# Expert slots padded to 128 instead of 256, in tiles of two halves, in a fused attention and mixture-of-experts layer

## The chip, the cores and the metric

The kernel runs on one NeuronCore of a Trainium2 chip, as one program and one launch. The metric is the device time of that program in microseconds. Before the change the median of three runs is 931.68 us (931.22 to 932.55). A difference is told here from medians; durations of single instructions come from one profiled execution, whose own time stands in the table below.

The core has four engines that matter here. [...] VectorE (DVE), ScalarE (ACT) and GpSimd (POOL) work element by element. Each runs its own queue of instructions in order, and waits on semaphores for the others. DMAs are issued from queues too: here almost all from SyncE's (SP), the ones with indices from POOL's.

## What is computed

The input x is 4 sequences of 1024 tokens of 128 channels, in float32. After a layer norm, an attention part and a mixture-of-experts part both read the normed rows xn, and both are added to x.

```python
x = x + attention(xn) + experts(xn)

# attention: 16 heads of 8 channels, each sequence of 1024
s = q @ k^T                                 # all columns, not only the causal ones
s = s - s.mean(-1); mad = abs(s).mean(-1) + 1e-6
s = s / mad * gain
r = max(where(causal, s, -1000), 0) ** 4
y = (r / (r.sum(-1) + 1e-6)) @ v;  y @ W_proj + b_proj

# experts: 8 experts, each token goes to its best 2, weights from a softmax over the two
z = (xn @ w1[e] + b1[e]) * (xn @ w2[e] + b2[e])          # 128 -> 256
y = silu(z @ wg[e] + bg[e]) @ w3[e] + b3[e]              # 256 -> 256 -> 128
```

There are 4096 tokens, so 8192 pairs of a token and an expert.

## The kernel before

**Order.** The program is written down by a planner (class `Plan`, before line 150). Every step (`add(...)`) names its engine or a choice of engines with a time each, the steps it depends on, the buffers it takes and gives back, and a rank. `Plan.run` repeatedly picks the step with the smallest start time, less a correction by name from the table `SOONER`, then by rank and the table `RANK`; so these tables, the times and the number of buffers of each kind (`kinds`) set the order of every engine's queue, and which engine takes a step that may run on several. Where PE would be idle, `pads` inserts a filler matmul (L1426). The order is fixed when the program is built; nothing is reordered when it runs.

**Attention.** For each of the 4 sequences (`prepare`), q and k are made channel by token (L767), and v token by channel (L873). q is scaled by a power of two that bounds it: L825 multiplies the absolute values of q by a matrix of mean absolute k, giving a bound in PSUM; L813 turns that into a power of two, written over the absolute values in SBUF (`aq`); L816 multiplies q by it. Sums of each head are then made from `aq` and q (L897, L903). k is copied four times with all but one quarter of the heads zeroed (`km`, L842). Then `chunk` handles 512 query rows at a time, two chunks in a sequence: `up` (L942) forms all scores, four heads at a time on 32 rows of the array each, whose absolute sums are drained by DVE (L955) or ACT (L957); `score` (L1066) forms the causal scores transposed, which go through a relu with the mask (L1085 on DVE; L1094 DVE, L1092 ACT), and two squarings (L1119 POOL, L1117 ACT); `relu` (L1133) and `values` (L1142) sum them and multiply by v, four heads on 32 columns of the array each; `finish` normalises, with a transpose (L1010).

**Routing.** `route` picks two experts for each token, counts the tokens of each expert, and gives each pair a slot: the slots of an expert begin at a multiple of TS = 256, so at most (8192 + 8 x 255) // 256 = 39 tiles of 256 slots are in use, and `owner` holds the expert of each tile. A 5 MB buffer in HBM (`xs`) is filled with zeros, and 64 indirect DMAs on POOL (L723) scatter the normed rows to their slots, with weight and destination beside each row.

**Experts.** `experts` goes through the 39 tiles. SP reads the tile's expert into a register and issues the rows (L1234) and the weights w1, w2, wg, w3 (L1235 to L1238), 640 KB, into one of two weight buffers. PE transposes the rows (L1247), multiplies by w1 and w2 (`up` of `experts`, L1257), ACT adds the bias (L1331), DVE adds the other bias and multiplies (L1339), PE multiplies by wg (`mix`, L1264), ACT applies silu (L1363), PE multiplies by w3 (`down`, L1273), DVE or ACT scales by the gate (L1285, L1288), and two indirect DMAs on POOL add the rows to a sum in HBM (L1293). A tile's down product and the next tile's up product are one step on PE, and so are its mix product and the next tile's transposes. These steps stand between the steps of the attention in PE's queue. At the end `collect` reads the sums back (L1381), adds them (L1390) and stores the output (L1395).

Of the kernel before, what the change touches and what calls it, by code (L numbers as in the profile page):

```python
# [9 lines left out]
I32 = mybir.dt.int32  # L10
# [16 lines left out]
TS = 256  # L27
# [24 lines left out]
class Plan:  # L52
# [6 lines left out]
    SOONER = {"score": 0.23, "mask": 0.1, "norm": 0.19, "tbias": -0.09, "count": -0.58, "v": 0.01, "top": 0.2, "wT": -0.06, "kappa": -0.11, "gateT": 0.12, "k": 0.21, "abs": -0.69, "ys": -0.51, "stats": 0.59, "exp": 0.14, "sq": -0.86, "bound": 0.53, "proj": -0.42, "least": 1.02, "xg": -0.51, "give": -0.32, "yT": -0.16, "sum": -0.3, "heads": 0.32, "gate": -0.5, "headsT": 0.15, "normal": 0.19, "second": -0.02, "relu": -0.88, "y@DVE": -0.32, "gate@DVE": 0.11, "relu@DVE": 0.45, "xT": 0.46, "xg@DVE": -0.05, "relu@ACT": 0.42, "out": -0.77, "yT@DVE": -0.19, "xT@DVE": -0.19, "place": -0.11, "gate@ACT": -0.01, "g": -0.01, "wT@ACT": 0.34, "heads@DVE": -0.33, "mean": -0.33, "y": -0.03, "abs@DVE": 0.6, "ys@DVE": -0.15, "sq@ACT": -0.11, "warm": 0.63, "xg@ACT": -0.83, "norm@ACT": 0.05, "up": 0.16, "q": 0.06, "blocks": -0.09, "ys@ACT": 0.01, "spill": -0.53, "weight": -0.46, "wT@DVE": 0.22, "gain": -0.07, "gates": 0.91, "av": -0.1}  # L59
    RANK = {"score": 221, "proj": -10, "yT": -194, "xg": -11, "sums": 48, "h": -24, "tbias": -35, "bound": -15, "top": 4, "headsT": 187, "spill": 12, "blocks": 240, "place": 4, "sum": -136, "std": -27, "gateT": 10, "count": -34, "scatter": 85, "xT": 210, "y": 196, "exp": 27, "second": -251, "load": 209, "relu": -111, "keys": 126, "mask": 6, "rows": -13, "scale": 8, "turn": 101, "wT": 23, "fill": 17, "ys": -19, "bias": -6, "g": -103, "give": -106, "gate": 36, "absq": 16, "norm": -137, "warm": -16, "v": -15, "hot": -162, "gates": 21, "stats": 20, "up": 78}  # L60
# [105 lines left out]
def layer_kernel(  # L166
# [49 lines left out]
    SB = TS // P  # L216
    N_TILES = (2 * NT + E * (TS - 1)) // TS
# [10 lines left out]
    def keep(shape, name, dtype=F32):  # L228
# [5 lines left out]
        "u": (8, [P, 2, CH]), "u1": (6, [P, 2, CH]), "blk": (14, [P, TB * WX]),  # L234
        "w": (2, [P, 2 * F + FB * F + FB * C]), "xg": (3, [P, SB, WX]), "xT": (2, [P, TS]),
        "z": (2, [P, FB, TS]), "s": (2, [P, FB, TS]), "ye": (2, [P, SB, C]),         "ys": (2, [P, CH]), "yt": (2, [P, CB, C]),
# [105 lines left out]
    tiles_f = keep([P, N_TILES], "tiles_f")  # L342
    expert_f = keep([P, 1], "expert_f")
    for t, pattern, base, cm in (
        (first, [[-1, E]], E, 0),
        (tiles_f, [[1, N_TILES]], 0, 0), (expert_f, [[0, 1]], 0, 1),
    ):
        nc.gpsimd.iota(t, pattern=pattern, base=base, channel_multiplier=cm, allow_small_or_imprecise_dtypes=True)
# [24 lines left out]
    xs = dram.tile([N_TILES * TS, WX], F32, name="xs")  # L373
# [47 lines left out]
    own = keep([E, N_TILES], "own")  # L421
    one8 = keep([P, TB], "one8")
    nc.vector.memset(one8, 1.0)
    owner = keep([P, N_TILES], "owner", I32)
    biases = keep([P, 3, FB, N_TILES], "biases")
# [130 lines left out]
    def route(rank):  # L556
# [84 lines left out]
        def owners(e):  # L641

            past = room(0, N_TILES * (E - 1)).rearrange("p (n e) -> p n e", e=E - 1)
            nc.vector.tensor_tensor(
                past, tiles_f.unsqueeze(2).to_broadcast([P, N_TILES, E - 1]),
                ends(1)[:, 1:].unsqueeze(1).to_broadcast([P, N_TILES, E - 1]), ALU.is_ge,
            )
            o0 = of_buf(k1)[:, NE + 160 : NE + 160 + N_TILES]
# [11 lines left out]
        def bias(e):  # L660
            pb = of_buf(k2)[:, : 3 * FB * N_TILES].rearrange("p (i f n) -> p i f n", i=3, f=FB)
            for i in range(3):
                for f in range(FB):
                    nc.tensor.matmul(pb[:, i, f, :], bes[:, i, f * P : (f + 1) * P], own, start=True, stop=True)
# [5 lines left out]
                biases.rearrange("p i f n -> p (i f n)"), of_buf(k2)[:, : 3 * FB * N_TILES]  # L670
# [72 lines left out]
    def prepare(b, cs, rank):  # L743
# [65 lines left out]
        def scale(here, bound):  # L809


            t = of_buf(aq)[:, here]
            nc.vector.tensor_scalar(  # L813
                t.bitcast(I32), bound.bitcast(I32), 0x7F800000, -0x1000000, ALU.bitwise_xor, ALU.bitwise_and
            )
            nc.vector.tensor_tensor(of_buf(qb)[:, here], of_buf(qb)[:, here], t, ALU.mult)  # L816

        sd = []
        for c in range(NC):
# [12 lines left out]
                    deps=[m, qd[c]], give=[k], rank=rank,  # L832
# [76 lines left out]
        m = add("heads", {"PE": 1.3}, heads, deps=sd + [bl], take=[sh[b]], give=[aq], rank=rank + 8)  # L909
# [305 lines left out]
    def experts(routed, ranks, stored):  # L1215
# [3 lines left out]
        tile_ = [{k: Buf(k) for k in ("w", "xg", "xT", "z", "s", "ye")} for _ in range(n_)]  # L1219

        def weights_of(i):
            w = of_buf(tile_[i]["w"])
# [4 lines left out]
        def loaded(i):  # L1227


            def load(e):  # L1230
                of_ = nc.sync.value_load(owner[0:1, i : i + 1], min_val=0, max_val=E - 1)
                this = bass.DynSlice(of_, 1)
                w1s, w2s, wgs, w3s = weights_of(i)
                nc.sync.dma_start(of_buf(tile_[i]["xg"]), slots_d[:, i * SB : (i + 1) * SB, :])  # L1234
# [224 lines left out]
```

## Time and profile before

| What | Value |
|---|---|
| Median of 3 runs | 931.68 us (931.22 to 932.55) |
| Profiled execution, its own time | 934.0 us |
| Its span, first to last instruction | 932.3 us |
| Granted TensorE clock, mean | 0.985 of full speed |
| PE, busy | 901.4 us |
| ACT, busy | 718.1 us |
| POOL, busy | 756.1 us |
| DVE, busy | 644.5 us |
| Moved by DMA | 58.63 MB, mean 63 GB/s |
| First expert tile's up product | 284.9 us after the start |
| Last expert tile's down product | 905.8 us |

Busy time is the union of an engine's instructions. PE's matmuls are pipelined and their records overlap, so what a burst of matmuls costs is read from its start to the start of the next one. A matmul of float32 operands stands in the trace as two records, a transpose as one. "32*128" in a record means 32 rows and 128 columns of the array; four such matmuls on different rows (or "128*32", different columns) run side by side. Line numbers are those of the kernel before; of the kernel after, its own.

### The profile page before, as it was taken

Reading aid. Unit: us, or ns where it says so; the run is one execution under the profiler, and the core shown is the slowest. Engines: PE = TensorE matmul, PEld = TensorE weight load, DVE = VectorE, ACT = ScalarE, POOL = GpSimd, SP = SyncE. Lnnn points to the kernel's source line nnn. Section 1 sums busy time; section 2 is a strip of 40 time slices with the busy share of each in tenths; the row PEclk is TensorE's granted clock in tenths of the full one; section 3 lists DMA queues with packets and bytes.
Section 4 is the critical chain, followed back from the end, with each engine's and each line's share of the span. In section 5 each row is a group of like instructions: output and inputs, shape, how many; then the busy total and the mean of one; then the engine's idle time right before and its main releaser. Section 6 shows DMA issues by size and latency. Waiting matters only on the chain.

```text
span 932.3 us, 20608 instructions
## 1 busy us (share of the span) xinstructions
PE 901.4 (97%) x7517; PEld 458.4 (49%) x7517; DVE 644.5 (69%) x1616; ACT 718.1 (77%) x1564; POOL 756.1 (81%) x519
## 2 busy tenths in 40 slices
PE   6899999998999999999899999999999999999996
PEld 4455433433454545545445654454545565544443
DVE  7888856568776766666567776665666776666565
ACT  5879888897786868678757877777787868678983
POOL 4478879889676889999957887999987838899992
PEclk9999999999898999999989999999999999999999
DMA  4820000000021233233212221232322222222106
GB/s 107 333 79 22 24 21 21 22 24 21 22 80 39 48 76 78 58 68 78 63 41 54 67 57 43 60 65 59 83 63 63 56 62 59 63 59 44 41 7 187
DMA packets 66275, 58.63 MB, mean 63 GB/s; under 512 B 6463, under 2 KB 62206, under 8 KB 66174
## 3 DMA queue, kind: packets, MB, share of 16 engines
q1 hardware_dynamic: 52168, 47.67, 16.8%
q0 software_dynamic: 13280, 9.38, 7.4%
q8 instruction: 59, 0.97, 0.4%
q10 hardware_dynamic: 726, 0.27, 0.2%
q14 instruction: 42, 0.34, 0.1%
HBM read 36.90 MB, written 20.40 MB: 61 GB/s over the span
## 4 chain that ended last, share of the span: by engine, by line
PE 83%; DVE 7%; POOL 6%; issue 2%; DMA 1%; ACT 1%; SPq 0%; ACTq 0%; POOLq 0%; DVEq 0%
PE bank L942 17%; PE bank L1066 16%; PE bank L1142 14%; PE bank L1133 9%; PE bank L1264 8%; PE bank L1257 7%; PE bank L1273 4%; POOL u L1119 4%; PE bank L1010 2%; POOL xs L723 1%; PE bank L767 1%; PE bank L1247 1%; DVE blk L816 1%; PE bank L1426 1%; DMA blk<-acc 1%
## 5 line engine op out<-in xcount | busy, mean ns | idle before, releaser
L1119 POOL TENSOR_TENSOR u<-u 128x1024 f32<-128x1024 f32 (+1 forms) x324 | 582.1, 1924 | 99.4 <-ACT u L1092 62.7
L1117 ACT ACTIVATE u<-u 128x1024 f32<-128x1024 f32 (+1 forms) x316 | 298.2, 971 | 11.7 <-POOL u L1119 5.6
L955 DVE TENSOR_REDUCE asum<-bank 128x1 f32<-128x512 f32 (+3 forms) x500 | 243.0, 543 | 62.1 <-PE bank L942 61.3
L1092 ACT ACTIVATE u<-bank 128x256 f32<-128x256 f32 (+2 forms) x355 | 152.4, 492 | 71.9 <-DVE u L1085 44.0
L942 PE MATMUL bank<-blk,blk 32*128 32x512 f32 (+3 forms) x1536 | 188.4, 529 | 7.1 <-DVE blk L816 4.7
L1085 DVE SCALAR_TENSOR_TENSOR u<-bank,causal 128x256 f32<-128x256 f32 (+1 forms) x384 | 121.2, 372 | 89.6 <-PE bank L1066 70.9
L1066 PE MATMUL bank<-blk,blk 32*128 32x512 f32 (+3 forms) x1536 | 178.9, 528 | 1.0 <-DVE u L1085 0.5
L1142 PE MATMUL bank<-u,V 128*32 128x512 f32 (+3 forms) x1536 | 165.1, 501 | 1.6 <-POOL u L1119 1.3
L957 ACT ACTIVATE bank<-bank 128x512 f32<-128x512 f32 (+3 forms) x268 | 130.5, 488 | 35.1 <-PE bank L942 31.8
L1293 POOL DMA_INDIRECT acc<-ye,xg x78 | 123.0, 1577 | 36.6 <-DVE ye L1285 20.5
L1094 DVE TENSOR_SCALAR u<-bank 128x512 f32<-128x512 f32 (+2 forms) x157 | 98.9, 656 | 55.9 <-PE bank L1066 55.9
L942 PEld LDWEIGHTS bank<-blk,blk 32*128 32x128 f32 x1536 | 90.6, 185 | 86.1 <-issue 13.5
L1133 PE MATMUL bank<-u,pick 128*32 128x512 f32 (+3 forms) x1280 | 129.1, 469 | 0.0
L1066 PEld LDWEIGHTS bank<-blk,blk 32*128 32x128 f32 x1536 | 65.7, 184 | 72.5 <-issue 27.1
L1133 PEld LDWEIGHTS bank<-u,pick 128*32 128x32 f32 x1280 | 43.6, 111 | 79.3 <-issue 74.5
L723 POOL DMA_INDIRECT xs<-blk,slot x64 | 64.5, 1008 | 21.4 <-DMA xs<-blk,slot 11.2
L1264 PE MATMUL bank<-z,w 128*128 128x256 f32 x312 | 77.1, 390 | 0.0
L1142 PEld LDWEIGHTS bank<-u,V 128*32 128x32 f32 x1536 | 33.9, 108 | 83.4 <-issue 58.3
L1257 PE MATMUL bank<-xT,w 128*128 128x256 f32 x312 | 74.7, 383 | 0.0
L1264 PEld LDWEIGHTS bank<-z,w 128*128 128x128 f32 x312 | 56.1, 190 | 25.9 <-issue 8.8
L1257 PEld LDWEIGHTS bank<-xT,w 128*128 128x128 f32 x312 | 56.9, 193 | 7.7 <-DVE asum L955 1.5
L1339 DVE SCALAR_TENSOR_TENSOR z<-bank,biases,z 128x256 f32<-128x256 f32 x78 | 37.2, 478 | 30.8 <-ACT z L1331 30.7
(176 smaller groups left out, 700.5 us busy)
## 6 DMA issues: line engine op xcount, KB each, us to landing
w<-in_L_ffn_w_dram SPq DMA_DIRECT2D x117, 128.0 KB
w<-in_L_ffn_wg_dram SPq DMA_DIRECT2D x39, 256.0 KB
xs<-w SPq DMA_DIRECT2D x1, 5070.0 KB
xg<-xs SPq DMA_DIRECT2D x39, 130.0 KB
acc<-w SPq DMA_DIRECT2D x1, 2048.0 KB
blk<-acc SPq DMA_DIRECT2D x4, 512.0 KB
out_dram<-xt SPq DMA_DIRECT2D x8, 256.0 KB
xt<-in_L_attn_x_dram SPq DMA_DIRECT2D x3, 512.0 KB
```

Source lines behind the costliest of these rows:

```text
L942: nc.tensor.matmul(of_buf(ks_[g])[:, at : at + w], of_buf(q[b])[rows_, ii * P : (ii + 1) * P], of_buf(km[b][r])[rows_, k0 : k0 + w], start ...
L955: nc.vector.tensor_reduce(to, of_, AX.X, ALU.add, apply_absolute_value=True)
L957: nc.scalar.activation(of_, of_, AF.Abs, accum_out=to)
L1066: nc.tensor.matmul(of_buf(ks_[g])[:, at : at + n], of_buf(km[b][r])[rows_, jj * P : (jj + 1) * P], of_buf(q[b])[rows_, c * CH + off : (c + ...
L1092: nc.scalar.activation(to, s_, AF.Relu)
L1117: nc.scalar.activation(to, s_, AF.Square)
L1119: (nc.vector if e == "DVE" else nc.gpsimd).tensor_tensor(to, s_, s_, ALU.mult)
L1133: nc.tensor.matmul(of_buf(acc)[32 * g : 32 * g + 32, off + lo : CH], pick, of_buf(u1s[g // 2])[:, g % 2, at + lo : at + n], start=begin, s ...
L1142: nc.tensor.matmul(of_buf(acc)[32 * g : 32 * g + 32, off:CH], of_buf(Vb[b])[:, jj, h0 : h0 + 32], of_buf(us[g // 2])[:, g % 2, at : at + n ...
L1257: nc.tensor.matmul(of_buf(k)[:, j * TS : (j + 1) * TS], wt[:, f * P : (f + 1) * P], of_buf(tile_[i]["xT"]), start=True, stop=True)
L1264: nc.tensor.matmul(of_buf(k)[:, g * TS : (g + 1) * TS], weights_of(i)[2][:, f, g * P : (g + 1) * P], of_buf(tile_[i]["z"])[:, f, :], start ...
L1293: nc.gpsimd.indirect_dma_start(out=acc_d, in_=of_buf(ye)[:, j, :], in_offset=None, compute_op=ALU.add, out_offset=bass.IndirectOffsetOnAxi ...
```

## The change

- TS becomes 128. A tile still has 256 slots, but in two halves (SB = 2) that may belong to different experts. There are at most 71 halves, so 36 tiles, and `owner`, `own`, `biases` and the zeroed buffer are sized by the 72 halves.
- Each half has weights and biases of its own: there are four weight buffers for two, a tile loads 2 x 640 KB, each 256-wide matmul of `up` and `mix` becomes two 128-wide ones with their own weights, and each instruction with a bias becomes two.
- Rows and weights are loaded by separate steps of the plan; the transpose waits for the rows alone, and the up product for the weights.
- In `scale`, the power of two is written in place in PSUM and multiplied into q from there; a new step copies it to `aq`, and the per-head sums wait for the copy.
- The kind "blk" has 11 buffers for 14, and the tables `SOONER` and `RANK` have other values, so that the whole program has another order, and some steps run on another engine.

```diff
-TS = 256
+TS = 128
-    SOONER = {"score": 0.23, "mask": 0.1, "norm": 0.19,
...
+    SOONER = {"score": 0.41, "v": 0.2, "wT": -0.2,
...
-    N_TILES = (2 * NT + E * (TS - 1)) // TS
+    SB = 2
+    TW = SB * TS
+    N_TILES = -(-((2 * NT + E * (TS - 1)) // TS) // SB)
+    N_OWN = N_TILES * SB
...
-        "u": (8, [P, 2, CH]), "u1": (6, [P, 2, CH]), "blk": (14, [P, TB * WX]),
-        "w": (2, [P, 2 * F + FB * F + FB * C]), "xg": (3, [P, SB, WX]), "xT": (2, [P, TS]),
+        "u": (8, [P, 2, CH]), "u1": (6, [P, 2, CH]), "blk": (11, [P, TB * WX]),
+        "w": (4, [P, 2 * F + FB * F + FB * C]), "xg": (3, [P, SB, WX]), "xT": (2, [P, TW]),
...
-            t = of_buf(aq)[:, here]
-            nc.vector.tensor_scalar(
-                t.bitcast(I32), bound.bitcast(I32), 0x7F800000, -0x1000000, ALU.bitwise_xor, ALU.bitwise_and
-            )
-            nc.vector.tensor_tensor(of_buf(qb)[:, here], of_buf(qb)[:, here], t, ALU.mult)
+            t = bound.bitcast(I32)
+            nc.vector.tensor_scalar(t, t, 0x7F800000, -0x1000000, ALU.bitwise_xor, ALU.bitwise_and)
+            nc.vector.tensor_tensor(of_buf(qb)[:, here], of_buf(qb)[:, here], bound, ALU.mult)
...
+            ts.append(
+                add(
+                    "bound", {"ACT": 0.58, "DVE": 0.62}, lambda e, k=k, here=here: copy(e, of_buf(aq)[:, here], of_buf(k)),
+                    deps=[sd[-1]], give=[k], rank=rank,
+                )
+            )
...
-        m = add("heads", {"PE": 1.3}, heads, deps=sd + [bl], take=[sh[b]], give=[aq], rank=rank + 8)
+        m = add("heads", {"PE": 1.3}, heads, deps=ts + [bl], take=[sh[b]], give=[aq], rank=rank + 8)
...
+            def rows_(e):
+                nc.sync.dma_start(of_buf(tile_[i]["xg"]), slots_d[:, i * SB : (i + 1) * SB, :])
+
             def load(e):
...
+                for j in range(SB):
+                    n = i * SB + j
+                    of_ = nc.sync.value_load(owner[0:1, n : n + 1], min_val=0, max_val=E - 1)
...
+            return (
+                add(
+                    "rows_in", {"SP": 0.6}, rows_, deps=routed, take=[tile_[i]["xg"]], rank=ranks[i] - 20, after=3.0,
+                    begin=max(0.0, ranks[i] - 20),
+                ),
+                add(
+                    "load", {"SP": 4.6}, load, deps=routed, take=tile_[i]["w"], rank=ranks[i] - 20, after=5.0,
+                    begin=max(0.0, ranks[i] - 20),
+                ),
+            )
...
         def up(i, f, k):
-            for j, wt in enumerate(weights_of(i)[:2]):
-                nc.tensor.matmul(
-                    of_buf(k)[:, j * TS : (j + 1) * TS], wt[:, f * P : (f + 1) * P], of_buf(tile_[i]["xT"]), start=True, stop=True
-                )
+            for m in range(2):
+                for j in range(SB):
+                    nc.tensor.matmul(
+                        of_buf(k)[:, m * TW + j * TS : m * TW + (j + 1) * TS], weights_of(i, j)[m][:, f * P : (f + 1) * P],
+                        of_buf(tile_[i]["xT"])[:, j * TS : (j + 1) * TS], start=True, stop=True,
+                    )
...
+                def first(e, i=i, f=f, k=k):
+                    for j in range(SB):
+                        at, n = slice(j * TS, (j + 1) * TS), i * SB + j
+                        nc.scalar.activation(
+                            of_buf(tile_[i]["z"])[:, f, at], of_buf(k)[:, at], AF.Identity, bias=biases[:, 0, f, n : n + 1]
+                        )
...
+                h = add("h", {"ACT": 0.46}, first, deps=[m] + zd[:1], rank=rank - 200)
+                zd.append(add("h", {"DVE": 0.46}, product, deps=[h], give=[k], rank=rank - 200))
...
-            s_ready = add("g", {"ACT": 0.74}, silu, deps=[m], give=[k], rank=rank - 200)
+            s_ready = add("g", {"ACT": 0.9}, silu, deps=[m], give=[k], rank=rank - 200)
```

The `mix`, product and silu steps are split into halves in the same way.

## The prediction

> **What bounds the kernel now.** I read the page first (shares, chain), then the stretches by time, then one expert tile in the timeline, and last the waits of TensorE.
>
> ```profile
> PE 901.4 (97%) x7517; PEld 458.4 (49%) x7517; DVE 644.5 (69%) x1616; ACT 718.1 (77%) x1564; POOL 756.1 (81%) x519
> ...
> PE 83%; DVE 7%; POOL 6%; issue 2%; DMA 1%; ACT 1%; SPq 0%; ACTq 0%; POOLq 0%; DVEq 0%
> ```
>
> TensorE is busy 97% of the span and is 83% of the chain that ended last; the rest of that chain is DVE and POOL, in places. Where these places are, the stretches tell (columns: stretch, its length, busy us and count of PE, PEld, DVE, ACT, POOL, granted clock, DMA share, GB/s):
>
> ```profile
> 67.00:125.00 58.00, 57.71 (x493) 29.07 (x490) 48.24 (x118) 51.46 (x129) 47.83 (x39) 1.00 0.07 22
> 125.00:217.00 92.00, 90.39 (x739) 33.83 (x735) 56.44 (x141) 79.19 (x153) 83.14 (x63) 1.00 0.07 22
> 217.00:290.00 73.00, 68.95 (x551) 33.99 (x547) 56.09 (x123) 55.52 (x127) 56.89 (x43) 0.91 0.15 44
> 290.00:457.00 167.00, 166.02 (x1388) 86.56 (x1381) 106.83 (x262) 125.00 (x262) 148.21 (x87) 1.00 0.29 67
> 457.00:477.00 20.00, 15.03 (x72) 7.80 (x70) 17.00 (x24) 10.09 (x18) 11.79 (x9) 0.83 0.17 34
> ...
> 600.00:906.00 306.00, 305.79 (x2622) 159.54 (x2619) 202.15 (x492) 240.03 (x514) 265.77 (x159) 1.00 0.26 57
> ```
>
> From 290 on, with expert tiles mixed in, PE is full and the others have room: there a microsecond of PE work is a microsecond of time. Before the first expert tile (284.9 us) ACT is at 89% (67 to 125) or POOL at 90% (125 to 217), and PE, though "busy", moves at their pace. Around 217 to 240 and 457 to 477, where a batch's q and k are prepared, PE stands still and its clock falls to 0.91 and 0.83.
>
> One expert tile on PE (start, length to the last end, line; x8 is four fp32 matmuls of two records each):
>
> ```profile
> 404.01 0.66 PE L1010 MATMUL bank<-ident,ys 128*128 128x128 f32 x4
> 404.50 1.89 PE L1264 MATMUL bank<-z,w 128*128 128x256 f32 x8
> 406.23 0.38 PE L1247 MATMUL bank<-ident,xg 128*128 128x128 f32 x2
> 406.55 1.14 PE L1066 MATMUL bank<-blk,blk 32*128 32x512 f32 x8
> 407.62 1.16 PE L1273 MATMUL bank<-w,s 128*128 128x128 f32 x8
> 408.61 1.89 PE L1257 MATMUL bank<-xT,w 128*128 128x256 f32 x8
> 410.43 0.71 PE L942 MATMUL bank<-blk,blk 32*128 32x256 f32 x8
> ```
>
> Read start to start. The eight 256-wide records of L1264 take 406.23 - 404.50 = 1.73 us, 0.216 each. L1257 takes 1.82: the extra 0.09 is the change to the 32-row form of L942. L1273's eight 128-wide records take 0.99; less 0.10 for the change before them that is 0.89, 0.111 each. A change of array form thus costs 0.1 to 0.2 us, leaving and entering.
>
> **The change, part by part.**
>
> *Fewer tiles, narrower matmuls.* Slots padded to 128: (8192 + 8 x 127) // 128 = 71 halves, so 36 tiles for 39. A tile now costs 0.89 (down) + 1.73 (up) + 1.73 (mix) + 0.22 (transposes) = 4.57 us; after, up and mix are 16 records of 128 each, 16 x 0.1115 = 1.78, and the tile 4.68. 39 x 4.57 = 178.2; 36 x 4.68 = 168.5: **-9.7 us**, all on PE, which has nothing to hide it behind. The doubt is the step of a 128-wide record with weights of its own. The row first: L1273 is that case already, a new stationary operand for each 128-wide matmul, at 0.111. [...] I take the row, since it is the same array, type and shape; between 0.108 and 0.115 the term lies between -13.7 and -5.7.
>
> *Replanned order.* In the built order of PE the changes of array form fall from 586 to 565 (rows to full array -10, columns to rows -12, columns from full -8, others +9). By the 0.1 to 0.2 us above, about 0.18 on average: **-3.8**. Filler matmuls are 16 for 17: nothing.
>
> *q times its power of two.* L816 multiplied two SBUF tiles; now the power of two is made in PSUM in place and the multiply reads it there, and a new copy (ACT or DVE) brings it to SBUF for the per-head sums.
>
> ```profile
> L816 DVE TENSOR_TENSOR blk<-blk,blk x8: 691/693/4174, 32.4 to 695.4; 128x512 f32<-128x512 f32 x8
> ...
> PE bank L942 <- DVE blk L816: 4.7, 2, 3.3
> ...
> 226.08 2.74 DVE blk L816
> ...
> 463.75 4.18 DVE blk L816
> ```
>
> Five of eight take 0.69 us, three take 2.74, 2.73 and 4.17, each beside a POOL square; L881 and L1208, of the same size with one operand in PSUM, average 0.68 and 0.69. So 2.05 + 2.04 + 3.48 = 7.6 us of DVE go. On PE: the 4.7 above, and 2.0 at 232.57 behind the second multiply, 6.7 in all. The halved clock that follows the standstills costs more: (1 - 0.83) x 20 = 3.4 at 457, (1 - 0.91) x 73 = 6.6 at 217. But the standstills have other causes too that stay (L797 2.51 us at 222.69, L805 2.82 at 458.92), so I credit little of that: **-8**, from -3 to -14. The eight copies of about 0.6 us (L435's 512-wide form 0.588, on ACT) are not ahead of the scores: only the per-head sums wait for them, and for these only the first head turn. What is late if they slip is that turn, and behind it the release of aq.
>
> *Rows apart from weights.* The built SP queue still runs rows, weights, weights, tile by tile, so a weight load still stands behind the rows' wait for an earlier scatter-add:
>
> ```profile
> SPq L1234 <- DMA acc<-ye,xg: 364.5, 36, 11.7
> ```
>
> Today this wait costs PE nothing: in the trace the rows of tile i+3 are issued 12 to 14 us after tile i's down product begins. In the new order the densest tiles are 12 to 14 us apart, and the transpose of those rows comes at the end of the mix of tile i+2, some 19 to 23 us after. Behind the rows come two weight sets, eight issues 0.58 us apart and two register loads of about 1 us: 6.7 us, so they start at about 13, end near 20 (the last waits for the next down product anyway) and are wanted at 26 or later. Bytes: 36 x 1.31 MB for 39 x 0.66, in the dense stretch 1.3 MB per 13 us = 100 GB/s more or less, where the second slice of the page moved 333. **0**, up to +2 for each of 22 dense tiles if scatter-adds come 6 us later than now.
>
> *Chain inside a tile.* Up to mix is ACT, DVE, ACT, DVE. Each 256-wide instruction (L1331 0.473, L1339 0.478) becomes two 128-wide ones with biases of their own: about 0.25 + 0.37 = 0.62 us a pair on ACT (0.473 less 128 elements at 0.83 ns, the slope between L957's forms of 512 and 128), 0.6 on DVE. [...] Now 9 us of other PE work lie between up and mix (410.43 to 419.86); in the built order of the changed kernel, with each burst at its duration in this trace, 14 of 36 tiles have just 2.6 to 3.5 us (a score, a value, a count and an up burst). A late mix holds everything behind it on PE. I take 0.3 to 0.4 us for those 14: **+5**, from 0 to +20.
>
> *Work moved to ACT.* In the built queues ACT gains 44 squares from POOL (31 of 1024, 0.95 start to start; 13 of 512, 0.52): 36 us; 82 absolute sums from DVE (0.27 for 128 to 0.60 for 512 with the read-out): 39; 20 relus: 8; and for the experts 288 x 0.25 for 156 x 0.36: 16. ACT goes from 718 to about 817 of some 920, 89%; POOL falls to about 665, DVE to about 600. In the first chunk (67 to 125), already the slowest, ACT gains about 2 us of work, while POOL, which paced 125 to 217, loses 7. Later stretches come to 85% on average, the fullest 25 us to some 95%. What waits when ACT is late is a PSUM bank, hence the next four-bank burst. 0 if the buffers even it out, +25 if ACT cannot pass the 89% it reaches at 67 to 125; nearer the former, as the 306 us from 600 ran with POOL at 87% and PE full: **+5**.
>
> *Fewer blk buffers (11 for 14), routing over 72 halves, later first tile.* DVE's placing of owners grows by 0.3 us; the tail after the last down product has the same structure. **0**, from -2 to +4.
>
> Sum: -9.7 - 3.8 - 8 + 5 + 5 = -11.5. The profiled execution took 934.0 (932.3 of span and 1.7 around it) and would become 922.5; the median of the runs lies 2.3 below it, so 931.7 becomes **920**.
>
> **Rivals.**
> 1. *The waits do not come* (chain and ACT at 0): 931.7 - 21.5 = 910. For it: the steady stretch has run without PE waits at POOL 87%. Against: the short gaps between up and mix.
> 2. *The waits eat the gain, no more*: 927 to 934. For it: first chunk, where ACT at 89% already slows PE.
> 3. *Slower: the mix waits.* Place: the mix of each tile, behind ACT's queue with 128-wide pairs. It pays 21.5 us back when the mean wait of 36 tiles reaches 0.6 us; at 0.9 it is 931.7 - 21.5 + 32 + 5 = 947. For it: ACT at 89%, strict order in its queue, a relu of 0.48 ahead of each pair. Against: 22 of 36 tiles have over 3.5 us.
> 4. *Weights or rows late* in the dense stretch, 2 us for 22 tiles: +44, about 964.
>
> **How the numbers follow.** Forecast (912 to 927 by itself) 0.58; rival 1 0.20; rival 2 0.10; rival 3 0.09; rival 4 0.03. A difference under 0.2%, 1.9 us, cannot be told from none here. Faster: 0.58 + 0.20 + about half of rival 2 = 0.83; same 0.04; slower 0.13. The range 906 to 933 leaves out rivals 3 and 4 and the ends of the others.
>
> **What would show it.** [...] It is wrong if PE's busy share drops below 95%, with ACT's u, z or bank releases named ahead of its waits, or DMA named ahead of the up products.

## The result, and the profile after

The changed kernel takes 923.36 us (median of four runs, 921.40 to 924.63) against 931.58 for the kernel before on the same chip: a ratio of 0.9908, 95% interval 0.9886 to 0.9930. A second measurement on another occasion gave 0.9927 (0.9910 to 0.9945). Where edits of the changed kernel are compared below, the mean of the two, 0.992, stands for it, which is 7.6 us less than before. The forecast was 920 with a range of 906 to 933.

The profiled execution took 921.4 us, span 919.7. First the busy times and the chain of its page, as they were shown of the kernel before:

```profile
PE 886.8 (96%) x8013; PEld 479.5 (52%) x8013; DVE 599.5 (65%) x1579; ACT 808.4 (88%) x1925; POOL 674.6 (73%) x469
...
PE 75%; ACT 9%; POOL 7%; DVE 5%; issue 2%; DMA 2%; ACTq 0%; DVEq 0%; POOLq 0%
```

TensorE (PE) is still the bound. ScalarE went from 718 to 808 us of work (forecast 817), GpSimd from 756 to 675 (665), VectorE from 645 to 600 (600). In the chain ScalarE's part rose from 1% to 9%.

Now the stretches (columns: stretch, its length, busy us and count of PE, PEld, DVE, ACT, POOL, granted clock, DMA share, GB/s):

```profile
69.00:126.00 57.00, 56.88 (x494) 30.22 (x494) 44.24 (x109) 53.95 (x141) 47.15 (x37) 0.97 0.06 19
126.00:215.00 89.00, 88.38 (x757) 32.89 (x757) 53.39 (x131) 84.24 (x172) 79.99 (x62) 1.00 0.07 23
215.00:289.00 74.00, 69.17 (x631) 35.82 (x627) 55.51 (x137) 66.03 (x164) 60.30 (x48) 1.00 0.15 48
289.00:451.00 162.00, 160.94 (x1490) 94.07 (x1491) 96.67 (x252) 146.94 (x337) 119.70 (x71) 1.00 0.47 119
451.00:477.00 26.00, 25.24 (x216) 16.68 (x219) 16.05 (x40) 21.54 (x47) 12.43 (x9) 1.00 0.56 141
...
600.00:906.00 306.00, 304.07 (x2890) 159.64 (x2883) 190.22 (x491) 279.56 (x652) 242.05 (x143) 1.00 0.27 66
```

Read them against the kernel before. A batch change is the place where the next sequence's q and k are prepared. In the second of those shown (457 to 477 there) PE was busy 15.0 of 20 us at a clock of 0.83; here, in 451 to 477, 25.2 of 26 at full clock. In the first (217 to 290 there) the clock was 0.91, and is 1.00. ScalarE is at 91% in 289 to 451 and from 600 on, where it had been at 75 and 78%; in 477 to 600 it is at 85%, for 80.

The means hide how the clock fell. In the kernel before it stood at one half in three places at the batch changes; in the changed kernel it is at full speed from 74.5 to 913 us. Three stretches of the kernel before, then one of the changed kernel:

```profile
232.00:238.60 6.60, 6.03 (x36) 2.28 (x40) 5.06 (x12) 1.63 (x3) 5.88 (x5) 0.50 0.07 23
279.80:286.40 6.60, 6.60 (x25) 2.85 (x24) 4.71 (x9) 4.95 (x17) 6.60 (x5) 0.50 0.11 29
467.60:474.20 6.60, 6.13 (x28) 1.94 (x32) 5.95 (x12) 1.29 (x4) 1.76 (x1) 0.50 0.33 70
...
74.50:913.00 838.50, 825.12 (x7577) 443.70 (x7572) 538.03 (x1366) 752.82 (x1795) 634.94 (x407) 1.00 0.31 79
```

One expert tile on PE:

```profile
406.87 1.16 PE L1294 MATMUL bank<-w,s 128*128 128x128 f32 x8
407.87 1.95 PE L1276 MATMUL bank<-xT,w 128*128 128x128 f32 x16
409.75 1.15 PE L1072 MATMUL bank<-blk,blk 32*128 32x128 f32 x16
...
413.75 2.05 PE L1285 MATMUL bank<-z,w 128*128 128x128 f32 x16
415.64 0.38 PE L1265 MATMUL bank<-ident,xg 128*128 128x128 f32 x2
415.95 0.50 PE L1072 MATMUL bank<-blk,blk 32*128 32x256 f32 x4
```

Start to start, the up burst takes 409.75 - 407.87 = 1.88 us, of which 0.10 is the change to the row form behind it, and the mix burst 415.64 - 413.75 = 1.89 with 0.11 for the change ahead of it: 1.78 each, as forecast. Record by record, both bursts step at 0.112 us in the median. There are 36 such tiles.

Last the multiply of q by its line (duration in ns: least, median, most), and then the list of waits (us in total, times, longest): TensorE's of the mix (PEld is its weight load) and for a DMA, and SyncE's of the rows:

```profile
L816 DVE TENSOR_TENSOR blk<-blk,bank x8: 686/689/689, 32.3 to 693.3; 128x512 f32<-128x512 f32 x8
```

```profile
PEld bank L1285 <- DVE z L1360: 5.5, 9, 0.8
...
PE bank L398 <- DMA rows<-in_L_attn_b_attn_dram: 4.8, 1, 4.8
...
PE bank L1285 <- DVE u L1091: 0.6, 2, 0.3
...
SPq L1237 <- DMA acc<-ye,xg: 207.5, 33, 8.0
```

All eight multiplies take 0.69 us. The mix waits 0.6 us in all, and not for z; its weight loads stand 5.5 us behind z (9 times, 0.8 at most), beside other matmuls that still run. The rows wait less for scatter-adds than they did (207.5 us for 364.5).

**Where the time went.** A busy share hides short waits, so I laid a ruler beside the trace: PE's instructions in built order, each at the step that the trace shows for its shape when nothing holds it, plus about 0.1 us for each change of array form. The trace's time less this sum is the lag, and grows where PE waits (before the first chunk also where the granted clock is below full: it is 0.94 from 12 to 41 us in the kernel before, and 0.81 in the changed one). That sum is 843.2 us for the kernel before and 831.1 for the changed one: **-12.1** of work, give or take 2, as the changed kernel has 1,120 more records of 128 columns on the full array, and their step lies between 0.109 and 0.112 us. The growth of the lag by stretch:

| stretch, about | before | changed | changed, second trace |
|---|---|---|---|
| 0 to 67 us (norms, first q and k) | 19.4 | 23.5 | 23.1 |
| 67 to 215 (attention alone) | 21.6 | 16.5 | 19.4 |
| 215 to 297 (first batch change, to the first tiles) | 20.5 | 15.9 | 15.3 |
| 297 to 445 (dense tiles) | 1.9 | 2.6 | 3.8 |
| 445 to 485 (second batch change) | 8.8 | 1.5 | 1.4 |
| 485 to 897 | 7.3 | 17.5 | 17.9 |
| sum | 79.5 | 77.5 | 80.9 |

So the gain is the 12 us of PE work. The batch changes gave 12 more and the stretch from 67 to 215 another 2 to 5; the start and the stretch after 485 took them back: 4 and 10. Behind PE's last instruction the changed kernel takes 9.0 us to its end, for 7.1 before. With the first trace that makes -12.1 - 2.0 + 1.9 = -12.2 of the 12.6 us by which the two spans differ.

Between these traces, most of the 12 us at the batch changes is the clock. In the three stretches at half clock the lag of the kernel before grows by 3.7, 3.3 and 3.1 us, 10 together, and the changed kernel has no such stretch there. The amount varies with the execution: between 215 and 485 us this trace has 20 us at half clock, and the two others of its order (experiments 1 and 2) 10 each; of the eight traces of the changed order without a new plan, five have none there and three (experiments 5, 9 and 10) 3.4. What brings the falls of the clock was not tried.

The two traces of the changed kernel differ by 3.6 us, all but 0.4 of it before 290 us. In the trace of experiment 11, whose edit plays no part before the tiles, the distance at 290 is 4.7. Two traces with one order of instructions can therefore be compared to about half a microsecond once the tiles have begun, and only to some 5 us before that.

### The profile page after: what moved, and what is told of

The parts are those of the page before. It is cut to its first block, busy times and chain, and to the rows that moved or that the text cites. A ratio compares the mean times of both kernels' runs of the same rounds, so it can differ in the third digit from the quotient of the medians.

```text
span 919.7 us, 22396 instructions
## 1 busy us (share of the span) xinstructions
PE 886.8 (96%) x8013; PEld 479.5 (52%) x8013; DVE 599.5 (65%) x1579; ACT 808.4 (88%) x1925; POOL 674.6 (73%) x469
## 4 chain that ended last, share of the span: by engine, by line
PE 75%; ACT 9%; POOL 7%; DVE 5%; issue 2%; DMA 2%; ACTq 0%; DVEq 0%; POOLq 0%
PE bank L948 14%; PE bank L1072 14%; PE bank L1148 13%; PE bank L1139 8%; PE bank L1285 7%; PE bank L1276 7%; POOL u L1125 5%; PE bank L1294 4%; ACT bank L963 3%; ACT u L1123 3%; ACT u L1098 2%; POOL xs L725 2%; PE bank L1016 2%; PE bank L769 1%; PE bank L825 1%
## 5 line engine op out<-in xcount | busy, mean ns | idle before, releaser
L1125 POOL TENSOR_TENSOR u<-u 128x1024 f32<-128x1024 f32 (+1 forms) x280 | 503.5, 1863 | 125.2 <-ACT u L1098 40.8
L1123 ACT ACTIVATE u<-u 128x1024 f32<-128x1024 f32 (+1 forms) x360 | 339.3, 972 | 8.7 <-POOL u L1125 4.2
L961 DVE TENSOR_REDUCE asum<-bank 128x1 f32<-128x512 f32 (+3 forms) x418 | 205.3, 548 | 56.6 <-PE bank L948 56.1
L1098 ACT ACTIVATE u<-bank 128x512 f32<-128x512 f32 (+2 forms) x375 | 161.7, 498 | 41.0 <-PE bank L1072 24.5
L1072 PE MATMUL bank<-blk,blk 32*128 32x512 f32 (+3 forms) x1536 | 181.4, 527 | 3.9 <-DVE u L1091 2.6
L948 PE MATMUL bank<-blk,blk 32*128 32x512 f32 (+3 forms) x1536 | 184.1, 524 | 0.2
L963 ACT ACTIVATE bank<-bank 128x512 f32<-128x512 f32 (+3 forms) x350 | 169.7, 487 | 15.3 <-PE bank L948 13.2
L948 PEld LDWEIGHTS bank<-blk,blk 32*128 32x128 f32 x1536 | 93.9, 185 | 75.3 <-DVE asum L961 11.8
L1100 DVE TENSOR_SCALAR u<-bank 128x512 f32<-128x512 f32 (+1 forms) x137 | 87.1, 666 | 50.2 <-PE bank L1072 48.3
L1072 PEld LDWEIGHTS bank<-blk,blk 32*128 32x128 f32 x1536 | 68.9, 184 | 67.3 <-issue 19.7
L1139 PEld LDWEIGHTS bank<-u,pick 128*32 128x32 f32 x1280 | 43.2, 110 | 77.6 <-issue 74.5
L1285 PEld LDWEIGHTS bank<-z,w 128*128 128x128 f32 x576 | 67.3, 191 | 19.4 <-DVE z L1360 5.5
L1285 PE MATMUL bank<-z,w 128*128 128x128 f32 x576 | 73.4, 281 | 0.6 <-DVE u L1091 0.6
L1360 DVE SCALAR_TENSOR_TENSOR z<-bank,biases,z 128x128 f32<-128x128 f32 x144 | 43.6, 345 | 42.1 <-ACT z L1353 30.7
L1276 PE MATMUL bank<-xT,w 128*128 128x128 f32 x576 | 70.3, 275 | 0.6 <-ACT u L1098 0.6
L963 ACT ACTIVATION_READ_ACCUMULATOR bank<-bank 128x1 f32 x350 | 68.2, 195 | 0.0
```

Source lines behind the costliest of these rows:

```text
L948: nc.tensor.matmul(of_buf(ks_[g])[:, at : at + w], of_buf(q[b])[rows_, ii * P : (ii + 1) * P], of_buf(km[b][r])[rows_, k0 : k0 + w], start ...
L961: nc.vector.tensor_reduce(to, of_, AX.X, ALU.add, apply_absolute_value=True)
L963: nc.scalar.activation(of_, of_, AF.Abs, accum_out=to)
L1072: nc.tensor.matmul(of_buf(ks_[g])[:, at : at + n], of_buf(km[b][r])[rows_, jj * P : (jj + 1) * P], of_buf(q[b])[rows_, c * CH + off : (c + ...
L1098: nc.scalar.activation(to, s_, AF.Relu)
L1123: nc.scalar.activation(to, s_, AF.Square)
```

## The experiments

Names: "changed kernel, order kept" means that only what a step emits is edited, so that the planner puts every step at the same place. An edit of costs, buffers, the number of tiles or the planner's tables makes it plan anew.

**1. Narrow matmuls alone (kernel before, order kept).**

```diff
-  nc.tensor.matmul(of_buf(k)[:, j*TS:(j+1)*TS], wt[:, f*P:(f+1)*P], of_buf(tile_[i]["xT"]), ...)
+  for h in range(SB):
+      nc.tensor.matmul(of_buf(k)[:, j*TS+h*P : j*TS+(h+1)*P], wt[:, f*P:(f+1)*P],
+                       of_buf(tile_[i]["xT"])[:, h*P:(h+1)*P], ...)      # the same in mix
```

> Kernel before, its order of instructions kept, 39 tiles: each 256-wide matmul of the up and the mix burst as two 128-wide ones with the same weights. My theory (a 128-wide record with a new stationary operand steps at 0.1115 us, 256-wide at 0.2157): 39 x (32 x 0.1115 - 16 x 0.2157) = +4.5 us, 936 us. [...] Rival (the step is hidden in slack): no change, 932.

935.97 us, ratio 1.0038 (1.0026 to 1.0051): +3.5 us. The same tile as the one shown of the kernel before, from this run:

```profile
404.79 1.95 PE L1267 MATMUL bank<-z,w 128*128 128x128 f32 x16
406.57 0.38 PE L1247 MATMUL bank<-ident,xg 128*128 128x128 f32 x2
...
408.95 1.95 PE L1258 MATMUL bank<-xT,w 128*128 128x128 f32 x16
410.83 0.71 PE L942 MATMUL bank<-blk,blk 32*128 32x256 f32 x8
```

Mix 1.78 for 1.73, up 1.88 for 1.82: 0.11 a tile, 39 x 0.11 = 4.3 us. From 291 to 902 us this trace falls behind that of the kernel before by 2.8. For these fp32 matmuls halving the width costs 3%.

**2. The multiply out of PSUM alone (kernel before, order kept).**

```diff
-  t = of_buf(aq)[:, here]
-  nc.vector.tensor_scalar(t.bitcast(I32), bound.bitcast(I32), 0x7F800000, -0x1000000, xor, and)
-  nc.vector.tensor_tensor(of_buf(qb)[:, here], of_buf(qb)[:, here], t, ALU.mult)
+  t = bound.bitcast(I32)
+  nc.vector.tensor_scalar(t, t, 0x7F800000, -0x1000000, xor, and)
+  nc.vector.tensor_tensor(of_buf(qb)[:, here], of_buf(qb)[:, here], bound, ALU.mult)
+  nc.vector.tensor_copy(of_buf(aq)[:, here], bound)
```

> Kernel before, its order kept: only q's multiply is changed, the power of two is made in PSUM in place, multiplied from there and then copied to SBUF on VectorE in the same step. My theory: three slow multiplies go from 2.7, 2.7 and 4.2 us to 0.69 and TensorE's standstill at the batch changes shrinks: -8 us (-3 to -14), 924 us. Rival (the standstills have other causes, and the copies of 0.6 us on VectorE eat the rest): -1 to -3, 929 to 931.

926.33 us, ratio 0.9927 (0.9904 to 0.9950): -6.8 us. The multiply's line, then the two batch changes in the columns of the stretches above, and last the first of them in the kernel before:

```profile
L814 DVE TENSOR_TENSOR blk<-blk,bank x8: 686/687/689, 32.4 to 689.7; 128x512 f32<-128x512 f32 x8
```

```profile
217.00:240.00 23.00, 21.54 (x164) 10.04 (x164) 18.65 (x37) 16.38 (x30) 20.91 (x17) 0.93 0.07 21
...
457.00:477.00 20.00, 18.35 (x131) 9.95 (x130) 15.96 (x31) 13.79 (x28) 15.04 (x10) 1.00 0.21 47
...
217.00:240.00 23.00, 18.99 (x134) 7.78 (x126) 18.26 (x25) 13.89 (x23) 21.02 (x16) 0.85 0.08 24
```

PE is busy 18.35 of 20 us at the second batch change, where it was 15.03 at a clock of 0.83. Laid beside the trace of the kernel before, this one gains 3.8 us between 214 and 235 us and 4.9 between 464 and 485, and less than 0.3 anywhere after: the step has its price and its places as forecast. What the price consists of is another matter. The clock is at full speed in the second batch change, and at one half for 3.4 us in this part of the first, where it had been for 6.8 (the stretch at 280 is still there); by the lag in these stretches some 5 of the 8.7 us between the two traces are clock, and the rest are standstills.

The multiply still meets GpSimd's squares here, and is not held by them:

```profile
462.30 3.62 POOL L1118 TENSOR_TENSOR u<-u 128x512 f32<-128x512 f32 x3
462.31 0.69 DVE L814 TENSOR_TENSOR blk<-blk,bank 128x512 f32<-128x512 f32 x1
```

**3. The multiply back in SBUF (changed kernel, order kept; the eight copies left out).** The diff of experiment 2 the other way, with the copy's step emitting nothing.

> Changed kernel, its order kept: the power of two goes to SBUF and the multiply reads two SBUF tiles as before; the eight copies are left out. My theory: the wins at the batch changes are those of this edit, +8 us (+3 to +14), 931 us against 923. Rival (they come from the new order, which has moved the squares of POOL away from the batch changes): +0 to +2, 923 to 925.

924.23 us, ratio 0.9912 (0.9892 to 0.9932): within 1 us of the changed kernel. The rival was right.

```profile
L818 DVE TENSOR_TENSOR blk<-blk,blk x8: 691/692/1675, 31.8 to 695.6; 128x512 f32<-128x512 f32 x8
```

The multiply reads two SBUF tiles again, and seven of eight stay near 0.69 us: in the new order only one of the eight stands beside GpSimd squares, two of 1.0 us, and that is the slowest, 1.68. After 290 us the distance between the two traces changes by under 0.5. So the edit and the new order cure the same ill, and either of them is enough: the edit is worth 6.8 us alone and nothing on top. (The copies that are left out here are some 4 us of other engines' work; the trace shows no gain from that.)

**4. The expert chain one instruction wide (changed kernel, order kept).** Bias, product and silu of a tile as 256-wide instructions with the biases of the first half, so the second half's own biases are left out.

```diff
-  for j in range(SB):
-      at, n = slice(j * TS, (j + 1) * TS), i * SB + j
-      nc.scalar.activation(z[:, f, at], of_buf(k)[:, at], AF.Identity, bias=biases[:, 0, f, n:n+1])
+  n = i * SB
+  nc.scalar.activation(z[:, f, :], of_buf(k)[:, :TW], AF.Identity, bias=biases[:, 0, f, n:n+1])
```

> Changed kernel, its order kept: bias, product and silu of a tile as one 256-wide instruction each with the first half's bias (the second half's own biases are left out). ScalarE loses 36 x (8 x 0.249 - 4 x 0.36) = 20 us of work and the chain from up to mix some 0.8 us. My theory (chain and ScalarE together cost 10 us): -4 to -8 us, 915 to 919. Rival 1 (the chain is covered by the 2.6 to 7 us of other work between up and mix, and ScalarE has room): no change, 923.

921.74 us, ratio 0.9884 (0.9860 to 0.9908), some 3 us less than 0.992, with overlapping intervals. The traces say it closer: from 300 us to the end it gains 1.5 us on the changed kernel, 1.3 of it between 466 and 610. ScalarE falls to

```profile
PE 885.8 (96%) x8013; PEld 479.1 (52%) x8013; DVE 590.9 (64%) x1507; ACT 789.3 (86%) x1781; POOL 674.5 (73%) x469
```

19 us less, and the chain is shorter in every tile, for 1.5 us of time. Neither the chain nor ScalarE's sum sets the pace by itself.

**5. ScalarE loaded further (changed kernel, order kept).**

```diff
-  for g in range(FB):
+  for g in [0, 1, 0, 1]:          # each silu of the tile twice, same values
```

> Changed kernel, its order kept: each silu of a tile is issued twice (same values), 36 x 4 x 0.249 = 36 us more of ScalarE, 808 to 844 us of busy time. My theory of the forecast (ScalarE's load already costs time, a stretch at 95% and more): +15 to +30 us, 938 to 953. Rival (buffers even it out up to full load): 923 to 928.

946.60 us, ratio 1.0149 (1.0128 to 1.0170): 2.3% or 21 us above the changed kernel, for 33 us more of ScalarE's busy time (36 worked out). The lag between the two traces grows tile by tile, 5.8 us over the 13 tiles from 300 to 466, 6.6 over the next 10, 7.8 over the last 12. The page's busy times, and two of TensorE's waits:

```profile
PE 902.6 (96%) x8013; PEld 483.1 (51%) x8013; DVE 599.3 (64%) x1579; ACT 841.6 (89%) x2069; POOL 675.4 (72%) x469
```

```profile
PE bank L1294 <- ACT s L1386: 3.2, 3, 2.1
PE bank L1072 <- DVE u L1091: 3.0, 4, 1.7
```

The down product now waits for silu in places. But that is not where the time goes: silu stands in a tile's own chain, and the edit makes this chain longer as well as ScalarE fuller, so I set the two traces side by side instruction by instruction. Of the 20.6 us by which this one falls behind from 300 to 897 us, 1.5 arise at the down product and 0.5 at the mix, and 16.0 at the attention's bursts of scores (12.6 at L948, 3.4 at L1072), which need PSUM banks (the kernel has eight such buffers of 128 x 512) that ScalarE or VectorE must empty first. VectorE's work is unchanged (599.3 us for 599.5). So it is ScalarE's queue that comes late, far more than the tile's chain. PE's busy time grew by 16 us with no work added: most of the waiting is inside what the records call busy. So the changed kernel sits at an edge: 19 us of ScalarE less bring 1.5 to 3, 33 us more cost 21.

**6. Tile count (changed kernel, replanned).**

```diff
-  N_TILES = -(-((2 * NT + E * (TS - 1)) // TS) // SB)     # 36
+  N_TILES = 39                                            # the last three hold no rows
```

> Changed kernel with 39 tiles of two halves for 36, replanned (the three more hold no rows). My theory (a tile costs TensorE 4.68 us and nothing hides it): +14.0 us, and 13 more changes of array form at 0.1, +1.3: 938 to 940 us against 923.4. Rival (tiles run in slack that TensorE has beside ScalarE's load): under +8, below 931.

941.80 us, ratio 1.0083 (1.0064 to 1.0102): 1.65% or 15.4 us above 0.992, where 15.3 had been worked out. Nothing hides a tile. This run was planned anew, but the lag on the ruler stays within 2 us of the changed kernel's second trace in every stretch, so the plan has little part in the 15.4.

**7. and 8. The planner's tables exchanged.** The changed kernel with the offsets and ranks of before, and the kernel before with the new ones (SOONER and RANK copied across, nothing else).

> Changed kernel, replanned with the planner's offsets and ranks of the kernel before; everything else of the change stays. Theory A (the new order's loss of 5 us of TensorE stalls before 69 us is the tables', while the multiply out of PSUM keeps the batch changes short): the loss goes, +0.6 for the changes of form: 918 to 920 us. Theory B (the new order is what shortens the batch changes; without it 4 to 8 us of standstill come back there): 924 to 928 us.

> Kernel before, replanned with the new offsets and ranks alone. If the order alone brings what the traces show between before and after (batch changes -8.5 us, the first 69 us +5, changes of form -0.7): 926 to 929 us. If the order is worth only its changes of form, as forecast: 931 to 932.

940.01 us, ratio 1.0076 (1.0060 to 1.0091), and 956.41 us, ratio 1.0259 (1.0240 to 1.0278). All theories missed: the old tables cost the changed kernel 15 us, and the new ones cost the kernel before 24. PE's work is nearly the same as under the own tables (831.7 for 831.1; 842.3 for 843.2); it is the waits. For the changed kernel under the old tables the lag's growth is 21.1 to 67 us, 22.2 to 210, 15.8 to 294, 4.1 to 437, 2.4 to 478 and 27.8 after it. The new tables thus save 3 to 6 us in the stretch to 215, where GpSimd's squares had set the pace, and 10 after 478, and cost 2 at the start. For the kernel before under the new tables, the first tile's up product comes at 333 us for 284.9, and more attention is left behind the last down product, 60 us to the end for 26; about 10 of the 24 us are more waiting there. What makes up the rest is not followed here.

In the last stretch of the changed kernel under the old tables there is one wait of a size of its own. TensorE's largest waits of that run, then its timeline around 690 us:

```profile
PE bank L825 <- DVE kapB L807: 7.5, 3, 6.6
```

```profile
683.40 11.19 POOL L1125 TENSOR_TENSOR u<-u 128x1024 f32<-128x1024 f32 x6
...
686.30 8.38 DVE L807 TENSOR_SCALAR kapB<-same,cstat,sign 128x128 f32<-128x128 f32 x1
...
694.74 3.59 PE L825 MATMUL bank<-blk,kapB 128*128 128x512 f32 x4 [6.58 <-DVE kapB L807]
```

An instruction of 0.35 us on VectorE, from SBUF to SBUF (it makes kapB, the matrix of mean absolute k), takes 8.38 us, and ends at 694.68, when a row of six GpSimd squares (683.40 + 11.19 = 694.59) ends. This looks like the ill of the multiply again, in an operation that the change did not move to PSUM. TensorE's 6.6 us behind it are nearly half of the 15 us; the rest of the last stretch, some 20 us of lag, is spread in small waits.

**9. and 10. Attention work moved off ScalarE (changed kernel, order kept).** The planner's step is emitted on another engine than planned:

```diff
+  MOVED = {"ACT": [701, 3830], "DVE": [709, 746, 1143, ...25 steps], "POOL": [1731, 1973]}
   for n in plan.run():
       if n.emit is not None:
-          n.emit(n.engine)
+          n.emit(getattr(n, "moved", n.engine))
```

> Changed kernel, its order kept, but 29 instructions of the attention between other engines: 25 of ScalarE's (relus and absolute sums) go to VectorE, 2 squares to GpSimd, 2 come back; ScalarE loses 10.5 us of work, VectorE gains 10.5. Theory (the small waits of score and up products after 486 us, 10 us more than before, are PSUM banks that wait for ScalarE just at these places): -3 to -5 us, 918 to 920. Rival (as with the 256-wide expert instructions, where 20 us less of ScalarE gave 2): 0 to -1, 922 to 923.

> As the run with 29 instructions moved, but with 176: 42 squares from ScalarE to GpSimd and 40 back at other places, 27 absolute sums and 25 relus to VectorE, 16 and 12 back, some copies. Theory: -5 to -8 us against the changed kernel, 915 to 918. Rival (one engine's lateness is traded for another's): within 2 us of it, 921 to 925.

29 steps: 925.61 us, ratio 0.9917 (0.9889 to 0.9946), no change, though ScalarE lost 8 us (808.4 to 800.6). 176 steps: 921.30 us, ratio 0.9867 (0.9843 to 0.9892), about 0.5% or 5 us below 0.992; the intervals just overlap with one of the changed kernel's two measurements and not with the other. Its trace doesn't bear out 5 us: from 290 to 895 us it gains about 1 on the changed kernel, and before 290, where traces of one order scatter, it lies 2 behind; the profiled execution, 923.2 us, was the slowest of its six. It has the lowest ratio of all runs here; whether by 1 or by 5 us is not settled.

**11. Rows and weights issued together (changed kernel, order kept).**

```diff
   def rows_(e):
-      nc.sync.dma_start(of_buf(tile_[i]["xg"]), slots_d[:, i * SB : (i + 1) * SB, :])
+      pass
   def load(e):
+      nc.sync.dma_start(of_buf(tile_[i]["xg"]), slots_d[:, i * SB : (i + 1) * SB, :])
```

> Changed kernel, its order kept, with the rows issued by the step that issues the weights (as in the kernel before), ahead of them. My forecast took the separation as worth 0: within 2 us, 922 to 925. Rival (rows that stand behind the wait for weight buffers come late for their transpose): 36 tiles x 0.3 to 1 us, 934 to 959.

926.50 us, ratio 0.9919 (0.9893 to 0.9945): no change. SyncE waits for the same things about as long as in the changed kernel (207.5 and 134.7 us there),

```profile
SPq L1240 <- DMA acc<-ye,xg: 211.1, 33, 8.6
SPq L1249 <- PE bank L1295: 133.2, 23, 12.0
```

and from 291 us to the end the trace moves by 0.1 us against that of the changed kernel.

**12. The changed kernel again**, as the reference of the edits.

> The changed kernel itself once more, as the reference of the edits made to it: 921 to 926 us, a ratio of 0.989 to 0.993 to the kernel before.

925.25 us, ratio 0.9927 (0.9910 to 0.9945).

## Why the prediction was right, and where it was not

*Fewer tiles, narrower matmuls (-9.7).* Right in size and cause. Records of one width taken alone sum to 764.4 us before and 754.0 after, -10.4; the narrow half costs +3.5 measured on 39 tiles (experiment 1), the three tiles 15.4 with their changes of form (experiment 6).

*Changes of array form (-3.8).* By the prices in the traces this is what they save, if a pass behind another of its form costs nothing more; the ruler credits 1.7 only. The trace of the kernel before has 589 changes of form, that of the changed kernel 568. A change adds 0.09 to 0.115 us to the last step of the old form, and to the first step of the new one 0.025 (columns) or 0.10 (rows, full array): 0.22 us from columns to rows, 0.21 from rows to the full array, 0.12 from the full array to columns. 12, 10 and 8 fewer of these, and 9 more of the others at 0.13 to 0.22, make the 3.8. I had priced a change at 0.18 us and no change at nothing. Where one burst in the row form follows another at 538.8 us of the kernel before, the four passes of 512 columns (a pass is four matmuls side by side, one record each) step at 0.533, 0.430, 0.429 and 0.538 us: those inside have no extra. Of ten such pairs in that trace five take 0.21 to 0.25 us over their width, the other five 0.35 to 2.0, and waits are not told apart there. The ruler puts 0.104 us on most passes in the row form, also behind another of that form; with 3.8 in place of 1.7 its -12.1 would be -14.2, at the edge of the 2 us that I gave it.

*q out of PSUM (-8).* Right as the price of the edit on the old order (-6.8, in the two places named), and the batch changes of the changed kernel did shrink by 12 us. Two things in it were wrong. I took the 6.7 us of standstill nearly whole and credited little of the clock; the traces say the reverse, with some 5 of 8.7 us clock in experiment 2, and 10 of the 12 between the traces of before and after. (The fall to 0.91 was also no even one: it was two stretches at one half, one of them at 280, behind the place that I had in mind.) And the attribution failed: I summed the edit and the new order as if they were independent, and experiment 3 shows that the order alone had already taken the squares away. The step should have asked of the built order where the squares stand.

*Rows apart from weights (0).* Right, by experiment 11 and by SyncE's waits.

*Chain inside a tile (+5).* The cost is not there. No run shows the 0.3 to 0.4 us in 14 tiles that make up the term, and in the kernel before VectorE follows ScalarE on this chain within 0.04 us (L1331 ends at 410.15, L1339 starts at 410.19). The 2.3 to 7 us of other work between up and mix were enough in all 36 tiles: the mix starts 0.1 to 0.7 us after the start of the record ahead of it, of which that record itself takes 0.1 to 0.54 (in the kernel before it starts 0.1 to 0.5 us after), and the shorter chain of experiment 4, with 19 us less on ScalarE, gave 1.5 us for both.

*Work moved to ScalarE (+5).* The sum of these two terms, +10, is what the lag after 297 us shows (+0.7 and +10.2), but the mechanism that I gave is not shown. On the ruler the waits sit inside the attention's bursts of scores after 485 us (`up`, L948, about 5 us, and `score`, L1072, about 4), 0.2 to 1.1 us each, at banks to be emptied. Were ScalarE's load their cause, then taking 19 us off it (experiment 4) or moving 8 (experiment 9) would have brought more than 1.5 and 0 (at the rate of experiment 5, 19 us would be worth some 12), and the changed kernel under the old tables, with ScalarE at 80%, would not have had some 20 us of lag there. What is shown is that there is no room for more (experiment 5). What makes up the 10 us stays open. That it goes with the order as a whole and not with one engine's load is what these runs suggest; none of them shows it.

*Before the first tile.* The forecast had no term for these stretches apart from the batch change. The new order loses 4 us up to 67, in both traces, in more short waits around the first q, k and gates (lag 23.5 and 23.1 for 19.4; under the old tables 21.1) and at a granted clock of 0.90 and 0.95, for 0.97 before. From 67 to 215 it gains 2 to 5, with GpSimd at 80 us of 89 where it had been at 83 of 92. These stretches scatter from trace to trace: by the means over the other traces of the two orders (experiments 1 and 2; 3 to 5, 9 and 11) the loss is nearer 2 us and the gain nearer 3.

*Buffers and routing (0).* Not tried by themselves: 11 for 14 blk buffers makes the planner plan anew, and experiments 7 and 8 show that such a run would measure the plan.

So the forecast held in part by its largest term, the tiles, and in part by luck: what it had too hopeful, the first 67 us by 2 to 4 (and by the ruler the form changes by 2), stood against batch changes that shrank by 12 for 8 and a better stretch to 215, and nothing in the working made these cancel. The forecast was made against the profiled execution, 934.0 to 922.5, and that execution of the changed kernel took 921.4; the medians moved by 8.2 only (7.6 by the mean of the two measurements), since the one profile of before lay 2.4 us above its median and that of the changed kernel 2 below. Rival 1 (no waits, 910) fell by the lag after 485; rival 2 (927 to 934) by the time alone, which lies 2 to 4 us below it; rival 3 (the mix waits) by the waits for z; rival 4 by TensorE's waits, where a DMA is named only once, at the start (4.8 us, L398), and by experiment 11. What I treated worst was the replanning: I priced the new order by its changes of form alone, while the tables and the kernel belong together to the amount of 15 to 24 us, more than any single edit here is worth. That did not show in the sum, as the tables were forecast with the kernel that they belong to.

## What to carry to other kernels

Where an order is planned, price an edit on the order that will run: two cures for one stall don't add, and an edit's value in the old order says little of its value in the new. Test an edit with the order kept, and test tables tuned for one kernel only with that kernel. An engine at 88% may show nothing when work is taken from it and still pass on 0.6 us of every microsecond added (ScalarE in experiments 9 and 5), so measure the slope in both directions before calling it the bound. And read the granted clock in short stretches: a mean of 0.91 over 73 us hid two stretches at one half, worth over 3 us each.

## What the hardware showed that I had not expected

An instruction on VectorE lasted through a whole row of GpSimd squares, not through one: 8.38 us for an instruction of 0.35, in experiment 7. At the four ends of a square within those 8 us (a square takes 1.87) it did not end; it ended 0.09 us after the last square of the row. In the traces such a meeting costs more the longer GpSimd's row is: 2.7 us beside one square of 1.91 and 4.2 beside three short ones of 3.62 together, both in the kernel before, and 8.4 here. What holds VectorE there was not tried by itself; in experiment 2 the multiply with one operand out of PSUM takes 0.69 us beside three squares.

Splitting a 256-wide fp32 matmul into two of 128, each with its own load of weights, cost 3% (1.78 us for 1.73). And a burst in the row form took 0.21 us over the width of its passes, the same for two passes (181 bursts in the trace of the kernel before) as for four (0.22, 53 bursts): it lies in the first and the last.

The half clock had a price that can be read off: in each of the three stretches of some 6.8 us that the kernel before spent at one half at its batch changes, the lag grew by 3.1 to 3.7 us, half of the stretch.
